# The last layer norm of a fused S5 and attention kernel: Newton's turns on ScalarE, product and sum on VectorE out of PSUM

## The chip, the cores and the metric

The kernel runs on one core of a Trainium2 chip. The metric is the device time of one execution in microseconds, the median of several runs. The engines are named as in the profile: PE (TensorE), PEld (its weight loads), ACT (ScalarE), DVE (VectorE), POOL (GpSimd) and SP (SyncE, which issues the DMAs here).

## The reference

Two sequences of 2048 rows and 512 features go through an S5 block with a feed-forward part, and then through one attention layer with 16 heads, after which comes the layer norm that is changed here. Cut to what matters:

```python
def _sln(h, w, ln_g, ln_b, Wg, bg, Wb, bb):
    mu = jnp.mean(h, axis=-1, keepdims=True)
    var = jnp.mean((h - mu) ** 2, axis=-1, keepdims=True)
    ln = (h - mu) / jnp.sqrt(var + EPS) * ln_g + ln_b
    gamma = (w @ Wg.T + bg)[:, None, :]
    beta = (w @ Wb.T + bb)[:, None, :]
    return gamma * ln + beta

h = _sln(hidden, ...)                       # first norm
q, k, v = ...                               # 16 heads of 32
energy = jnp.einsum('bhqd,bhkd->bhqk', q, k)
att = jax.nn.softmax(energy, axis=-1) / D ** 0.5
out = (att @ v) @ Wp.T + bp
h1 = out + hidden
h2 = _sln(h1, ...)                          # the last norm
return h2 + h1
```

With g = gamma * ln_g and t = gamma * ln_b + beta the last step is, for each row, h1 + t + g * (h1 - mean) / sqrt(var + eps).

## The kernel before

**Attention in blocks and steps.** After the S5 part (about 1.47 ms) attention runs in 64 blocks: 2 batches, 8 pairs of heads, 4 chunks of 512 queries. A block has NP = 8 steps, and step j of the whole loop (j = 8 times the block, plus the step) handles two of the block's 16 key tiles. Ten of the 16 are computed 15 steps ahead (AHEAD): PE writes scores `s` (L754), ACT copies them to a ring (L765, `keep`), DVE keeps their running maximum (L770). The six others only give a maximum at first (`across`: PE m, DVE top L784) and are computed again when they are used (`make`: PE s, DVE adds the shift, pT L819). The negated maximum of each query, `shift`, is turned by PE (`turn_run`, L790 and L791, at steps 2 and 4 of a block; `spread`, L801 and L803, at step 5) and comes back through DRAM. POOL adds it to the kept tiles (`take_off`, L813), ACT takes the exponential (L824), and PE multiplies with v (L834, `weighted`) a step later. PSUM has two buffers `s`, one `m`, one `o` and one bank `pt`, which the turned maxima share with the last part below.

**The last part of the layer** is done per tile of 128 rows, four tiles to a chunk. `fetch` loads the heads' outputs, the divisors and the residual rows; `divide` (POOL, L892) divides; `project` (PE, L905) multiplies with Wp; `residual` (DVE, L911) adds, which gives h; `statistics` (DVE, L917 and L920) takes mean and variance. `deviation`, for two tiles at once (128x2 operands), computes 1/sqrt(var + eps) on DVE: v (L932), a first guess from the bits (L119), three Newton turns of three instructions (L124, L126, L127), and the shift -mean * scale (L938). `last_norm` is an activate on ACT, y = scale * h + shift. `close` on POOL multiplies by g and adds h + t, which `add_t` has left ready (L924, L962, L963), and SP stores the rows.

**Which step it falls in.** The order on every engine is that of the program, which `after(j, ...)` (at the start of step j) and `closing(j, ...)` (at its end, j + 0.5) fill by hand. Batch 0's 16 tiles are worked off while batch 1's attention runs, two in every three blocks: the even tile of a pair starts in one block and the odd one in the next. Their projection uses the bank `pt`. Batch 1 (LB, the last one) has its first three chunks, 12 tiles, at the end of the loop, one tile in every two steps; there the projection uses `m`, and last_norm writes to PSUM (z, L949), DVE multiplies by g (L950), POOL adds t and then the product (L960, L963). Batch 1's last chunk is the tail, `end_last`: four tiles at once, after the last block.

**The tail.** After the projection into py and statistics on DVE, ACT copies py to `hts` (L1057), POOL adds t to each of the four (L1059), while DVE computes the deviations of all four (128x4, L1063 and `rsqrt`). ACT normalises into SBUF (L1069), DVE multiplies by g (L1073), and the sums with hts (L1074) go to DVE and POOL in turn.

Of the kernel before, what the change touches and what calls it, by code (L numbers as in the profile page):

```python
# [8 lines left out]
F32 = mybir.dt.float32  # L9
# [3 lines left out]
I32 = mybir.dt.int32  # L13
AF = mybir.ActivationFunctionType
ALU = mybir.AluOpType
# [4 lines left out]
P = 128  # L20
EPS = 1e-5
# [18 lines left out]
def tile_s5_block_then_sln_attention(  # L40
# [21 lines left out]
    nc = tc.nc  # L62
    NB, L, D = x.shape
    KC = D // P
    CH = 512
    TT = CH // P
# [8 lines left out]
    const = ctx.enter_context(tc.tile_pool(name="const", bufs=1))  # L75
    small = ctx.enter_context(tc.tile_pool(name="small", bufs=2))
# [10 lines left out]
    nc.gpsimd.memset(cond_q, 0.0)  # L87
    nc.gpsimd.tensor_copy(cond_q[:, :, :NB], cond)
    four = const.tile([P, NB], F32, name="four")

    mod = const.tile([P, N_MOD, KC, NB], F32, name="mod")
    u_scale = const.tile([P, KC, NB], F32, name="u_scale")
# [20 lines left out]
        return vec[:, at : at + KC].unsqueeze(2).to_broadcast([P, KC, NB])  # L113


    def rsqrt(v, y, n, turns=(0, 3)):

        if turns[0] == 0:
            nc.vector.tensor_scalar(  # L119
                y.bitcast(I32), v.bitcast(I32), -0.5, float(0x5F3759DF), ALU.mult, ALU.add  # L120
            )
        for _ in range(*turns):
            a = small.tile([P, n], F32, name="rs_a", tag=f"rs_a{n}")
            nc.vector.tensor_mul(a, y, y)  # L124
            b = small.tile([P, n], F32, name="rs_b", tag=f"rs_b{n}")
            nc.vector.scalar_tensor_tensor(b, a, -0.5, v, ALU.mult, ALU.mult)  # L126
            nc.vector.scalar_tensor_tensor(y, b, 1.5, y, ALU.add, ALU.mult)  # L127
# [725 lines left out]
    held, ending = {}, {}  # L853
# [54 lines left out]
    def residual(b, qt):  # L908

        o4, h, py = held[b, qt]  # L910
        nc.vector.tensor_add(h, py, h)  # L911
        held[b, qt] = h, o4.rearrange("p g q -> p (g q)")

    def statistics(b, qt):
        h, ht = held[b, qt]
        st = small.tile([P, 6], F32, name="st3")
        nc.vector.bn_stats(st, h)  # L917
        if qt % 2 == 0:
            held[b, "mv"] = small.tile([P, 2, 2], F32, name="mv3")
        nc.vector.bn_aggr(held[b, "mv"][:, qt % 2, :], st)  # L920

    def add_t(b, qt):
        h, ht, *_ = held[b, qt]
        nc.gpsimd.tensor_tensor(ht, h, ending[b][1], ALU.add)  # L924

    def deviation(b, qt, parts=(0, 1)):

        mv = held[b, "mv"]
        if 0 in parts:
            v = small.tile([P, 2], F32, name="v3")  # L930
            y = small.tile([P, 2], F32, name="scale3", bufs=3)
            nc.vector.tensor_scalar(v, mv[:, :, 1], EPS, None, ALU.add)  # L932
            held[b, "vy"] = v, y
        v, y = held[b, "vy"]
        rsqrt(v, y, 2, {(0,): (0, 1), (1,): (1, 3), (0, 1): (0, 3)}[tuple(parts)])
        if 1 in parts:
            shift = small.tile([P, 2], F32, name="shift3", bufs=3)
            nc.vector.scalar_tensor_tensor(shift, mv[:, :, 0], -1.0, y, ALU.mult, ALU.mult)  # L938
            for i in range(2):
                h, ht = held[b, qt - 1 + i]  # L940
                held[b, qt - 1 + i] = h, ht, y[:, i : i + 1], shift[:, i : i + 1]

    def last_norm(b, qt):

        h, ht, scale, shift = held[b, qt]
        y = work.tile([P, D], F32, name="y")
        if b == LB:
            z = ps.tile([P, CH], F32, name="z", tag="pt")
            nc.scalar.activation(z, h, AF.Identity, bias=shift, scale=scale)  # L949
            nc.vector.tensor_tensor(y, z, ending[b][0], ALU.mult)  # L950
        else:
            nc.scalar.activation(y, h, AF.Identity, bias=shift, scale=scale)
        held[b, qt] = h, ht, y

    def close(b, qt):

        h, ht, y = held.pop((b, qt))
        if b == LB:
            ht = h
            nc.gpsimd.tensor_tensor(h, h, ending[b][1], ALU.add)  # L960
        else:
# [68 lines left out]
    def end_last(o):  # L1030
        raw, inv, on = (spare(n)[:, 0, :] for n in ("raw4", "inv4", "on4"))
        turned = ps.tile([P, 2, 2 * P], F32, name="turned", tag="pt")
        parts = [slice(2 * i * P, 2 * (i + 1) * P) for i in range(2)]
        for at in parts:
            nc.scalar.copy(raw[:, at], o[:, at])
        end_begin(1)
        for i, at in enumerate(parts):
            nc.tensor.matmul(turned[:, i, :], ends["turn"], raw[:, at], start=True, stop=True)  # L1038
        for i, at in enumerate(parts):
            nc.vector.reciprocal(inv[:, at], turned[:, i, :])  # L1040
            nc.vector.tensor_tensor(on[:, at], o[:, at], inv[:, at], ALU.mult)
# [24 lines left out]
        for t in range(TT):  # L1066
            qt = LC * TT + t
            y, ht = ends["h"][t // 2][:, t % 2, :], hts[t // 2][:, t % 2, :]
            nc.scalar.activation(  # L1069
                y, ends["py", t // 2][:, t % 2, :], AF.Identity,  # L1070
                bias=shift[:, t : t + 1], scale=scale[:, t : t + 1],
            )
# [38 lines left out]
    FIRST = -AHEAD - 8  # L1111
    OPEN = -4
    for i, n in enumerate(opens):
        free = NP * (max(m for m in range(N) if pair_of[m] == i - 2) + 1) if i > 1 else FIRST
# [2 lines left out]
    for n in range(N):  # L1117
        after(max(FIRST + 1 + n, NP * n - AHEAD - 6), load_q, n)
        after(NP * n - AHEAD + NP + 1, turn_run, n, 0)
        after(NP * n - AHEAD + NP + 3, turn_run, n, 1)  # L1120
        after(NP * n - AHEAD + NP + 4, spread, n)
    for b in range(NB):
        for c in range(NQ):
            j = NP * (blocks.index((b, NPAIR - 1, c)) + 1) + 1
# [21 lines left out]
            for t in range(TT):  # L1146
                qt = c * TT + t
                if b == LB:
# [30 lines left out]
    def run_due(j):  # L1179
        for what, args in due.pop(j, ()):  # L1180
# [117 lines left out]
```

## Time and profile before

| | |
|---|---|
| median of 3 runs | 3531.95 us (3527.56 to 3532.42) |
| the profiled execution | 3530.68 us, of which the span of the instructions is 3528.9 us |
| mean granted clock of TensorE | 0.983 |
| busy in the span | PE 96%, DVE 63%, ACT 54%, POOL 57% |
| attention and the last part | from about 1472 us to the end |
| batch 0's last part | blocks 34 to 58, about 2455 to 3264 us |
| batch 1's twelve tiles | about 3324 to 3497 us |
| the tail | about 3497 us to the end |

A line of a window names its stretch in us from the start of the span, its length, the busy time and number of instructions of PE, PEld, DVE, ACT and POOL, then the granted clock, the DMA share and GB/s. A line of the timeline has the start, the busy time, engine, line, operation, tiles, shapes and number of instructions merged, and in brackets the idle time of the engine before it with what ended it. A line of a group ends with the busy time, the mean in ns of one instruction, and the idle time before the group.

### The profile page before, as it was taken

The page shows a single profiled execution, that of the slowest core. Times are in us where ns is not written, and L with a number is a line of the kernel's source. Part 1 is how long each engine was busy: PE and PEld are TensorE (multiplying, and loading weights), DVE is VectorE, ACT ScalarE, POOL GpSimd, SP SyncE. Part 2 cuts the span into 40 slices and gives each one's busy share as a digit, 9 for nine tenths or more (in the row PEclk, how much of TensorE's full clock was granted, in tenths as well). Part 3 has the DMA queues.
Part 4 walks back from the last instruction along what each step waited for, and adds up shares of the span by engine and source line. Part 5 has one row for each costly group of instructions (what it writes and reads, how often), then busy time and mean ns, then how long its engine had stood idle before and what let it go on. Part 6 is the DMA issues. An engine that isn't in the chain of part 4 may idle for free. (4 is left out here: it accounts for less than half of the span.)

```text
span 3528.9 us, 34023 instructions
## 1 busy us (share of the span) xinstructions
PE 3382.5 (96%) x11772; PEld 1536.7 (44%) x11772; DVE 2219.1 (63%) x2946; ACT 1899.6 (54%) x2150; POOL 2006.8 (57%) x1028
## 2 busy tenths in 40 slices
PE   7999999999999999899999999999999999999986
PEld 4444444444444444444444444444444444444432
DVE  6233232323232212589999999998888888888865
ACT  2111112111111111488888888888788888888743
POOL 4223131313131311288877888888798888888765
PEclk8999999999999999999999999999999999999988
DMA  8001111111111012332313222232233323323232
GB/s 298 1 30 42 48 39 45 39 49 38 48 36 42 33 43 75 100 71 65 71 48 76 70 66 63 55 72 67 71 83 85 90 71 79 84 71 79 72 92 78
DMA packets 201539, 236.91 MB, mean 67 GB/s; under 512 B 89754, under 2 KB 118938, under 8 KB 197272
## 3 DMA queue, kind: packets, MB, share of 16 engines
q1 hardware_dynamic: 201368, 234.74, 24.4%
q8 instruction: 93, 1.52, 0.2%
q14 instruction: 78, 0.64, 0.1%
HBM read 166.77 MB, written 67.76 MB: 66 GB/s over the span
## 5 line engine op out<-in xcount | busy, mean ns | idle before, releaser
L813 POOL TENSOR_TENSOR x<-x,shift 128x1024 f32<-128x1024 f32 x640 | 1506.6, 2396 | 237.3 <-DMA shift<-flat 177.1
L765 ACT COPY x<-s 128x1024 f32<-128x1024 f32 x640 | 635.3, 1013 | 291.5 <-PE s L754 288.9
L754 PE MATMUL s<-qs,ks 128*128 128x512 f32 x2048 | 699.6, 432 | 48.1 <-DVE run L770 44.3
L824 ACT ACTIVATE x<-x 128x1024 f32<-128x1024 f32 x640 | 676.8, 1058 | 16.5 <-POOL x L813 16.5
L834 PE MATMUL o<-x,v 128*64 128x512 f32 x2560 | 673.4, 622 | 0.6 <-ACT x L824 0.6
L770 DVE TENSOR_TENSOR run<-s,run 128x1024 f32<-128x1024 f32 x512 | 625.2, 1221 | 56.6 <-ACT x L765 39.0
L819 DVE TENSOR_TENSOR pT<-s,shift 128x1024 f32<-128x1024 f32 x384 | 467.5, 1217 | 57.9 <-PE s L754 52.6
L784 DVE TENSOR_REDUCE top<-m 128x1 f32<-128x768 f32 x512 | 486.0, 949 | 25.7 <-PE m L779 25.3
L754 PEld LDWEIGHTS s<-qs,ks 128*128 128x128 f32 x2048 | 346.4, 189 | 303.9 <-DVE run L770 133.2
L488 PE MATMUL ph<-fT,w_sb 128*128 128x512 f32 x1024 | 462.4, 596 | 0.0
L501 PE MATMUL po<-w_sb,hid 128*128 128x512 f32 x1024 | 460.3, 592 | 0.0
L824 ACT ACTIVATE pT<-pT 128x1024 f32<-128x1024 f32 x384 | 407.6, 1061 | 59.2 <-DVE pT L819 51.8
L834 PE MATMUL o<-pT,v 128*64 128x512 f32 x1536 | 399.4, 598 | 13.4 <-ACT pT L824 13.4
L492 ACT ACTIVATE hid<-ph,vec 128x512 f32<-128x512 f32 x128 | 88.1, 688 | 594.8 <-PE ph L488 594.8
L159 DVE SCALAR_TENSOR_TENSOR lo<-pk,vec,hi 128x512 fp32r<-128x512 f32 x64 | 48.1, 751 | 502.7 <-ACT hi L158 497.5
L488 PEld LDWEIGHTS ph<-fT,w_sb 128*128 128x128 f32 x1024 | 192.9, 191 | 228.2 <-issue 228.2
L779 PE MATMUL m<-ks,qs 128*128 128x384 f32 x1024 | 286.1, 361 | 5.2 <-DVE top L784 3.5
L501 PEld LDWEIGHTS po<-w_sb,hid 128*128 128x128 f32 x1024 | 190.7, 190 | 221.5 <-issue 221.5
L435 POOL TENSOR_TENSOR m<-m,m 128x512 f32<-128x512 f32 x8 | 13.1, 1644 | 448.5 <-DVE m L433 448.5
L834 PEld LDWEIGHTS o<-x,v 128*64 128x64 f32 x2560 | 140.1, 137 | 265.2 <-issue 163.0
L158 ACT ACTIVATE hi<-pk,vec 128x512 fp32r<-128x512 f32 x64 | 44.0, 688 | 392.5 <-PE pk L531 392.5
L511 POOL TENSOR_TENSOR x<-x,gated 128x512 f32<-128x512 f32 x32 | 39.6, 1271 | 354.3 <-DVE gated L510 354.3
(249 smaller groups left out, 2844.9 us busy)
## 6 DMA issues: line engine op xcount, KB each, us to landing
ks<-kd SPq DMA_DIRECT2D x128, 256.0 KB
qs<-qd SPq DMA_DIRECT2D x512, 64.0 KB
shift<-flat SPq DMA_DIRECT2D x64, 512.0 KB
x<-in_x SPq DMA_DIRECT2D x8, 1024.0 KB
w_sb<-in_w SPq DMA_DIRECT2D x8, 1024.0 KB
x<-x SPq DMA_DIRECT2D x8, 1024.0 KB
kd<-hi SPq DMA_DIRECT2D x32, 256.0 KB
kd<-lo SPq DMA_DIRECT2D x32, 256.0 KB
```

The source lines that it names most:

```text
L488: nc.tensor.matmul(ph, w1_sb[:, k, f * P : (f + 1) * P], fts[b, c][:, k, :], start=k == 0, stop=k == KC - 1)
L492: nc.scalar.activation(hids[f], ph, AF.Gelu_apprx_tanh, bias=vec[:, V_B1 + f : V_B1 + f + 1], scale=1.0)
L501: nc.tensor.matmul(pos[b, c][:, t, :], hid[:, t * P : (t + 1) * P], w2_sb[:, f, :], start=f == 0, stop=f == FC - 1,)
L754: nc.tensor.matmul(s[:, e, :], kst[pair_of[n], e][:, kt * P : (kt + 1) * P], qst[n][:, e, :], start=True, stop=True,)
L765: nc.scalar.copy(x, s)
L770: nc.vector.tensor_tensor(runs[n], s, kept[n, 0] if kt == 1 else runs[n], ALU.max)
L779: nc.tensor.matmul(m[:, i, :YW], qst[n][:, e, t * P : (t + 1) * P], kst[pair_of[n], e][:, k : k + YW], start=True, stop=True,)
L784: nc.vector.tensor_reduce(tops[n][:, j, 0:1], m[:, :, :YW], AX.XY, ALU.max, negate=True)
L813: nc.gpsimd.tensor_tensor(x, x, shifts[n], ALU.add)
L819: nc.vector.tensor_tensor(x, s, shifts[n], ALU.add)
L824: nc.scalar.activation(x, x, AF.Exp)
L834: nc.tensor.matmul(outs[n][64 * e : 64 * e + 64, :], v[:, kt, e : e + 2, :], x[:, e, :], start=first, stop=final,)
```

## The change

`deviation` and `add_t` go. `statistics` now also computes, per tile on 128x1 operands, v = var + eps, the first guess `y` of the root, v * -0.5, and -mean, all four on DVE. A new function `newton` does the turns on ACT, as three activates each (y squared; times v plus 1.5; times y), and at the end multiplies -mean by the root. `last_norm` writes z to the bank `pt` for every tile. A new function `gain` has DVE multiply z by g in PSUM and add h. `close` keeps one addition on POOL, of t. The steps of these calls are set anew, one tile at a time. `SPREAD` only gives a name to the step at which `spread` already is. In the tail the normalised rows stay in PSUM, DVE multiplies and adds, and t is added last, by POOL for three tiles and by DVE for the fourth.

```diff
     def statistics(b, qt):
...
+        v = small.tile([P, 1], F32, name="v3")
+        y = small.tile([P, 1], F32, name="scale3", bufs=4)
+        shift = small.tile([P, 1], F32, name="shift3", bufs=4)
+        nc.vector.tensor_scalar(v, mv[:, 1:2], EPS, None, ALU.add)
+        nc.vector.tensor_scalar(
+            y.bitcast(I32), v.bitcast(I32), -0.5, float(0x5F3759DF), ALU.mult, ALU.add
+        )
+        nc.vector.tensor_scalar(v, v, -0.5, None, ALU.mult)
+        nc.vector.tensor_scalar(shift, mv[:, 0:1], -1.0, None, ALU.mult)
+        held[b, qt] = h, y, shift, v
+
+    def newton(b, qt, turns, final):
+
+        h, y, shift, v = held[b, qt]
+        for _ in range(turns):
+            c = small.tile([P, 1], F32, name="c3")
+            nc.scalar.activation(c, y, AF.Identity, scale=y)
+            nc.scalar.activation(c, c, AF.Identity, bias=one_half, scale=v)
+            nc.scalar.activation(y, c, AF.Identity, scale=y)
+        if final:
+            nc.scalar.activation(shift, shift, AF.Identity, scale=y)
 
     def last_norm(b, qt):
...
+        h, scale, shift, _ = held[b, qt]
+        z = ps.tile([P, CH], F32, name="z", tag="pt")
+        nc.scalar.activation(z, h, AF.Identity, bias=shift, scale=scale)
+        held[b, qt] = h, z
+
+    def gain(b, qt):
+
+        h, z = held[b, qt]
+        nc.vector.tensor_tensor(z, z, ending[b][0], ALU.mult)
+        nc.vector.tensor_tensor(h, z, h, ALU.add)
 
     def close(b, qt):
 
-        h, ht, y = held.pop((b, qt))
-        if b == LB:
-            ht = h
-            nc.gpsimd.tensor_tensor(h, h, ending[b][1], ALU.add)
-        else:
-            nc.gpsimd.tensor_tensor(y, y, ending[b][0], ALU.mult)
-        nc.gpsimd.tensor_tensor(y, y, ht, ALU.add)
-        nc.sync.dma_start(out[b, qt * P : (qt + 1) * P, :], y)
+        h, z = held.pop((b, qt))
+        nc.gpsimd.tensor_tensor(h, h, ending[b][1], ALU.add)
+        nc.sync.dma_start(out[b, qt * P : (qt + 1) * P, :], h)
...
             nc.scalar.copy(hts[i], ends["py", i])
-            for t in range(2):
-                nc.gpsimd.tensor_tensor(hts[i][:, t, :], hts[i][:, t, :], t_row, ALU.add)
...
         for t in range(TT):
+            z = ends["py", t // 2][:, t % 2, :]
+            nc.scalar.activation(
+                z, z, AF.Identity, bias=shift[:, t : t + 1], scale=scale[:, t : t + 1]
+            )
+        for t in range(TT):
             qt = LC * TT + t
...
-            nc.vector.tensor_tensor(y, y, g_row, ALU.mult)
-            (nc.gpsimd if t % 2 else nc.vector).tensor_tensor(y, y, ht, ALU.add)
+            y, z = hts[t // 2][:, t % 2, :], ends["py", t // 2][:, t % 2, :]
+            nc.vector.tensor_tensor(z, z, g_row, ALU.mult)
+            nc.vector.tensor_tensor(y, z, y, ALU.add)
+            (nc.gpsimd if t < TT - 1 else nc.vector).tensor_tensor(y, y, t_row, ALU.add)
...
                     after(k + 3, statistics, b, qt)
-                    if t % 2:
-                        after(k + 4, deviation, b, qt)
-                        after(k + 5, last_norm, b, qt - 1)
-                        closing(k + 5, last_norm, b, qt)
-                        after(k + 6, close, b, qt - 1)
-                        closing(k + 6, close, b, qt)
+                    closing(k + 3, newton, b, qt, 2, False)
+                    closing(k + 4, newton, b, qt, 1, True)
+                    closing(k + 4, last_norm, b, qt)
+
+                    (after if (k + 5 - SPREAD) % NP == 0 else closing)(k + 5, gain, b, qt)
+                    closing(k + 6, close, b, qt)
                 else:
...
                     closing(k + 7, statistics, b, qt)
-                    after(k + 9, add_t, b, qt)
-                    if t % 2:
-                        closing(k + 8, deviation, b, qt, (0,))
-                        closing(k + 9, deviation, b, qt, (1,))
-                        closing(k + 10, last_norm, b, qt - 1)
-                        closing(k + 11, last_norm, b, qt)
-                        after(k + 12, close, b, qt - 1)
-                        after(k + 14, close, b, qt)
+                    for i in range(3):
+                        closing(k + 8 + i, newton, b, qt, 1, i == 2)
+
+                    k += 2 if t % 2 else 8
+                    closing(k + 10, last_norm, b, qt)
+                    closing(k + 11, gain, b, qt)
+                    after(k + 13, close, b, qt)
```

In batch 0 k is step 3 of the tile's own block. The turns of a tile stand at the ends of steps 3, 4 and 5 of the block after its own. The two z of a pair stand in the same block, the one after the odd tile's own: the even tile's at the end of step 5, the odd tile's at the end of step 7. Each gain stands one step behind its z.

More of the change, by code (lines that the diff above doesn't have):

```diff
@@ L89, in tile_s5_block_then_sln_attention @@
     four = const.tile([P, NB], F32, name="four")
+    one_half = const.tile([P, 1], F32, name="one_half")
+    nc.gpsimd.memset(one_half, 1.5)
     mod = const.tile([P, N_MOD, KC, NB], F32, name="mod")
@@ L113, in per_feature, with rsqrt @@
         return vec[:, at : at + KC].unsqueeze(2).to_broadcast([P, KC, NB])
[L116 to L122, printed above, removed]
+    def rsqrt(v, y, n):
+        nc.vector.tensor_scalar(
+            y.bitcast(I32), v.bitcast(I32), -0.5, float(0x5F3759DF), ALU.mult, ALU.add
+        )
+        for _ in range(3):
             a = small.tile([P, n], F32, name="rs_a", tag=f"rs_a{n}")
@@ L911, in residual @@
         nc.vector.tensor_add(h, py, h)
-        held[b, qt] = h, o4.rearrange("p g q -> p (g q)")
+        held[b, qt] = h
     def statistics(b, qt):
-        h, ht = held[b, qt]
+        h = held[b, qt]
         st = small.tile([P, 6], F32, name="st3")
         nc.vector.bn_stats(st, h)
[L918 to L941, printed above, removed]
@@ L943, in last_norm @@
-    def last_norm(b, qt):
-        h, ht, scale, shift = held[b, qt]
-        y = work.tile([P, D], F32, name="y")
-        if b == LB:
-            z = ps.tile([P, CH], F32, name="z", tag="pt")
-            nc.scalar.activation(z, h, AF.Identity, bias=shift, scale=scale)
-            nc.vector.tensor_tensor(y, z, ending[b][0], ALU.mult)
-        else:
-            nc.scalar.activation(y, h, AF.Identity, bias=shift, scale=scale)
-        held[b, qt] = h, ht, y
-    def close(b, qt):
-        h, ht, y = held.pop((b, qt))
-        if b == LB:
-            ht = h
-            nc.gpsimd.tensor_tensor(h, h, ending[b][1], ALU.add)
-        else:
-            nc.gpsimd.tensor_tensor(y, y, ending[b][0], ALU.mult)
-        nc.gpsimd.tensor_tensor(y, y, ht, ALU.add)
-        nc.sync.dma_start(out[b, qt * P : (qt + 1) * P, :], y)
+        mv = small.tile([P, 2], F32, name="mv3")
@@ new lines, in statistics @@
+        nc.vector.bn_aggr(mv, st)
+        v = small.tile([P, 1], F32, name="v3")
+        y = small.tile([P, 1], F32, name="scale3", bufs=4)
+        shift = small.tile([P, 1], F32, name="shift3", bufs=4)
+        nc.vector.tensor_scalar(v, mv[:, 1:2], EPS, None, ALU.add)
+        nc.vector.tensor_scalar(
+            y.bitcast(I32), v.bitcast(I32), -0.5, float(0x5F3759DF), ALU.mult, ALU.add
+        )
+        nc.vector.tensor_scalar(v, v, -0.5, None, ALU.mult)
+        nc.vector.tensor_scalar(shift, mv[:, 0:1], -1.0, None, ALU.mult)
@@ L1066, in end_last @@
         for t in range(TT):
-            qt = LC * TT + t
[L1068 to L1072, printed above, removed]
-            nc.vector.tensor_tensor(y, y, g_row, ALU.mult)
-            (nc.gpsimd if t % 2 else nc.vector).tensor_tensor(y, y, ht, ALU.add)
+            z = ends["py", t // 2][:, t % 2, :]
+            nc.scalar.activation(
+                z, z, AF.Identity, bias=shift[:, t : t + 1], scale=scale[:, t : t + 1]
+            )
+        for t in range(TT):
+            qt = LC * TT + t
+            y, z = hts[t // 2][:, t % 2, :], ends["py", t // 2][:, t % 2, :]
+            nc.vector.tensor_tensor(z, z, g_row, ALU.mult)
+            nc.vector.tensor_tensor(y, z, y, ALU.add)
+            (nc.gpsimd if t < TT - 1 else nc.vector).tensor_tensor(y, y, t_row, ALU.add)
             nc.sync.dma_start(out[LB, qt * P : (qt + 1) * P, :], y)
@@ L1111, in tile_s5_block_then_sln_attention @@
     FIRST = -AHEAD - 8
+    SPREAD = -3
     OPEN = -4
@@ L1120, in tile_s5_block_then_sln_attention @@
         after(NP * n - AHEAD + NP + 3, turn_run, n, 1)
-        after(NP * n - AHEAD + NP + 4, spread, n)
+        after(NP * n + SPREAD, spread, n)
     for b in range(NB):
```

## The prediction

> **What bounds the kernel now.** I read the page first: PE is busy 96% of the span, GpSimd only 57%, so shortening GpSimd's work is worth something only where PE waits for it, directly or through another engine. Next the windows, one block of attention each: an undisturbed block, then the blocks with the even tile's projection, the odd tile's projection, and the end of the pair's last norm.
>
> ```profile
> 2225.30:2254.10 28.80, 28.27 (x123) 12.82 (x122) 26.19 (x27) 25.71 (x28) 23.51 (x10) 1.00 0.15 42
> 2682.80:2714.70 31.90, 31.57 (x130) 14.27 (x129) 27.17 (x30) 25.91 (x28) 28.22 (x14) 1.00 0.58 128
> 2714.70:2746.90 32.20, 30.49 (x126) 13.39 (x124) 27.33 (x34) 25.90 (x28) 25.91 (x12) 1.00 0.14 38
> 2746.90:2778.70 31.80, 30.38 (x127) 13.56 (x127) 29.01 (x35) 27.09 (x30) 26.21 (x14) 1.00 0.46 96
> ```
>
> The columns after the length are busy PE, PEld, DVE, ACT, POOL. A clean block takes 28.8 us with PE busy for all but 0.5 of it; a projection adds 3.05 us of PE. So the third window should take 31.85 and the fourth, which has no projection, 28.8: it takes 31.8. Counted from one first L784 of a block to the next in DVE's timeline, the eight blocks that hold a pair's norm take 32.07 (2732.21 to 2764.29) to 34.74 us, 33.15 on average, 4.36 more than a clean one: 35 us in batch 0. The even tile's block takes 32.12.
>
> Then the groups and DVE's timeline, for what costs so much. v (L932) is a 128x2 instruction of 0.15 us that takes 1.38 on average:
>
> ```profile
> L932 DVE TENSOR_SCALAR v<-mv 128x2 f32<-128x2 f32 x12 | 16.5, 1377 | 0.0
> ...
> 3403.07 7.00 POOL L813 TENSOR_TENSOR x<-x,shift 128x1024 f32<-128x1024 f32 x3
> ...
> 3404.49 0.97 DVE L932 TENSOR_SCALAR v<-mv 128x2 f32<-128x2 f32 x1
> ...
> 3405.50 2.28 DVE L119 TENSOR_SCALAR scale<-v 128x2 int32<-128x2 int32 x1
> ...
> 3407.82 2.27 DVE L124 TENSOR_TENSOR rs_a<-scale 128x2 f32<-128x2 f32 x1
> ...
> 3410.13 0.16 DVE L126 SCALAR_TENSOR_TENSOR rs_b<-rs_a,v 128x2 f32<-128x2 f32 x1
> ...
> 3413.08 1.06 ACT L824 ACTIVATE pT<-pT 128x1024 f32<-128x1024 f32 x1 [7.25 <-DVE pT L819]
> ...
> 3414.19 1.08 PE L834 MATMUL o<-pT,v 128*64 128x512 f32 x4 [2.92 <-ACT pT L824]
> ```
>
> Each of these DVE instructions ends where a GpSimd instruction ends (7.00/3 = 2.33 us each); when GpSimd is out of work, the next one takes 0.16. Behind the chain stands pT, and ACT and PE stand behind pT.
>
> The third thing is how tightly a clean block is coupled. PE writes a tile of scores s, ACT copies it (L765), DVE takes the running maximum (L770), and only then PE may write that buffer again. The step with two copies, from the timeline of a clean block:
>
> ```profile
> 2220.98 1.93 ACT L765 COPY x<-s 128x1024 f32<-128x1024 f32 x2 [0.29 <-PE s L754]
> 2222.02 2.55 DVE L770 TENSOR_TENSOR run<-s,run 128x1024 f32<-128x1024 f32 x2
> ...
> 2223.30 0.73 PE L754 MATMUL s<-qs,ks 128*128 128x512 f32 x2
> ...
> 2224.63 0.72 PE L754 MATMUL s<-qs,ks 128*128 128x512 f32 x2 [0.25 <-DVE run L770]
> ```
>
> The first run starts as its copy ends (2220.98 + 1.01), and each s of PE starts as a run ends. ACT idled only 0.29 us before. What is put ahead of that copy on ACT, or ahead of that run on DVE, delays PE almost one to one; elsewhere in the block ACT has 0.3 to 0.8 us a step.
>
> **What the Trainium skill says.** "GPSIMD Engine Reference", 1. Specifications: GpSimd shares its SBUF interfaces with VectorE, which shows with instructions in a 2-port mode or with two SBUF inputs. The trace agrees: L119 and L124 wait out GpSimd, while L911, L819 and L770 (one input in PSUM) keep 0.68 and 1.2 us beside it. "ScalarE: Activation LUTs", What ACT_TABLE_LOAD costs: 186 ns plus 0.833 ns an element, about 93 ns for each [128,1] pointer operand. L952 with two pointers agrees (price 0.80, trace 0.805 us). "TensorE: Matmul & The Clock Gate", Part 1: the array's clock drops after idle windows; the windows after 3400 us show 0.82 to 0.88.
>
> **The change, part by part.** PE's order is the same before and after.
>
> 1. *Deviation leaves DVE.* Per pair go 12 small instructions, 11 x 0.195 (0.16 and a gap of 0.035) = 2.15 and v's 1.38. Per tile come four 128x1 ones (v, first guess, -0.5 v, -mean): 4 x 0.19 = 0.76. The trace has no 128x1 tensor_scalar beside GpSimd; the nearest is last (L453), a 128x1 copy beside L461, 0.15 us, with no wait. Bounds 0.6 to 8 us a tile; I take 0.76.
>
> 2. *Newton on ACT.* Three dependent 128x1 activates a turn, with one, two and one pointers: 0.28 + 0.37 + 0.28, plus gaps of 0.035 as on DVE: about 1.03 us, an estimate from the skill's price; 0.28 more for the last shift. No such row is in the trace; bounds 0.7 and 1.6 a turn. 28 tiles x 3.4 = 95 us more on ACT, of which most falls on idle ACT, but not all: see 5.
>
> 3. *Product and sum on DVE out of PSUM.* Two of 0.69 us (L950 has 690 ns) per tile, neither with two SBUF inputs. They hold the one pt bank from z on; the next user is turn_run at least half a step later, so I see no wait there.
>
> 4. *GpSimd* keeps one of three 1.29 us instructions a tile: 16 x 2.58 + 12 x 1.27 = 57 us less. Worth nothing in batch 0: GpSimd runs ahead there and stands 9.2 us per pair for y (L962); it will stand for the gain instead, some 4 us later in the block, with two more take_offs done before. On SP as many out-DMAs as before (0.3 us each) wait for it, the odd tile's now behind the next fetch; loads have steps to spare.
>
> 5. *Batch 0, even tile's block* (now 32.12 us). The step counted is the one with two copies. Its first copy starts 10.14 us into a clean block (2220.98 less 2210.84). In the step before, pT now comes behind residual, statistics and the four small ones, so the exp behind it ends at about 9.8 (before 9.2); then turn 1 of 1.03 and the next exp of 0.96: copy at 11.8. Run L770 is then 1.65 us later than in a clean block instead of 0.43, and PE's next s starts when it ends. The later turns fall into steps with a projection, where ACT has 1.3 us spare. Loss 1.2 us x 8 = 10.
>
> 6. *Odd tile's block* (now 33.15). The same 1.65; then turn 2 and turn 3 with shift and the even z (0.77) overrun ACT's slack in steps 5 and 6 by about 1.3; the even gain (1.38 less slack) delays step 8 by about 1.2. The odd gain falls where DVE waits 1.27 us for pt_run and costs nothing; without that cover it costs 1.4. Sum 4.1 to 4.2 against 4.36 now: -0.2 x 8 = -2. Batch 0 together: **+8 us**, from -10 to +20.
>
> 7. *Batch 1's twelve tiles* (3324 to 3497 us). From residual (L911) to residual a tile takes 11.1 to 17.0 us. While scores are still kept (five tiles, 68.1 us), the chain is projection 3.7, then DVE: residual 0.69, statistics 0.87, small 0.76, pT 1.13, top 0.86, run 1.15, gain 1.3, pT and top 2.0: 12.5 a tile, -5.5. Afterwards (six, 79.5 us) the intervals with a deviation take 13.2 to 17.0 and two without 10.2. I take 11.3, since exp now stands behind statistics and two turns (2.1 us): -11.7. The last pair's stall: -2. Together **-19**, from -8 to -27.
>
> 8. *Tail.* L1059's adds go, and with them the waits of v, guess, rs_a and rs_b: 0.28 + 1.02 + 1.02 + 1.02 = 3.35 us. Then z 0.81, eight DVE instructions of 0.65, one add of 0.69 after GpSimd's third: the last sum ends at 3522.1 instead of 3525.9: **-3.8**.
>
> Sum: 8 - 19 - 3.8 = -15. The profiled execution took 3530.68 (span 3528.9 and 1.8 around it); the median shown is 1.3 above. So 3531.95 - 15 = **3517**.
>
> **Rivals.**
> - *Slower: ACT's turns decide.* The place is L765 behind a turn in batch 0, the price 4 turns' worth per pair (one in the even block, three in the odd) x 8 = 32 us for each 1 us that a turn takes over 1.03. From 1.5 us a turn nothing is left of the 15; at 1.7 it is slower by over 7. For it: ACT is 89% busy in a clean block. Against: the price of pointers fitted L952. At 1.8: 3541.
> - *Slower by far: 128x1 tensor_scalars wait for GpSimd too.* Three waits of 2.3 us and half a one, 8 us a tile, 16 tiles: near 3640. L453 speaks against it.
> - *Faster than I say.* Row slack swallows ACT's turns (as the even block swallowed 1.56 us of residual and statistics for 0.41): batch 0 at -10, batch 1 at -25: 3493.
> - *Nothing to measure.* Projection, residual and the m bank set batch 1's pace whatever DVE does (two intervals without a deviation took 14.4 and 14.9): -8 there, -3.8, +8: 3528.
>
> **How the numbers follow.** A measurement of this kernel tells about 0.2% (7 us) from no change. My forecast (3503 to 3525) 0.45, faster than that 0.22, nothing 0.15, ACT's turns 0.12, tensor_scalar waits 0.06. So faster 0.67, same 0.15, slower 0.18. The range 3494 to 3541 leaves out the far rival and the ends.
>
> **What would show it.** c, scale and shift as 128x1 rows on ACT near 0.3 us; v at 0.15 us with GpSimd running; blocks of batch 0 near 33.3 and 32.9 us; residuals of batch 1 at most 13 us apart; no GpSimd in the 8 us before the last z. Wrong would be v near 1.4 us or more, ACT waited for by run L770 throughout batch 0 with blocks over 35, or residuals still 14 apart.

## The result, and the profile after

The kernel after takes 3533.14 us (median of 20 runs, 3529.99 to 3535.05); the kernel before, run beside it, 3529.53 us (20 runs). The ratio is 1.0009, with a 95% interval from 1.0002 to 1.0016: 3 us slower, where the forecast was 15 faster. The profiled span went from 3528.9 to 3531.7 us. Measured on the two traces, part by part (a step starts with its first exponential on ACT):

| | predicted | measured | from |
|---|---|---|---|
| batch 0's last part | +8 | +8.5 | first top (L784, after: L785) of block 36 to the start of step 487: 855.98 and 864.5 us |
| batch 1's twelve tiles | -19 | -3.0 | start of step 487 to start of step 511: 162.3 and 159.3 us |
| the end | -3.8 | -3.7 | start of step 511 to the end: 37.2 and 33.6 us |

The first top of block 36 also comes 1.0 us later (2474.3 us in place of 2473.3), ahead of everything that was changed in attention; in the traces of all runs below it lies between 2472.0 and 2476.1. So two rows were met in their sums, and the row of batch 1 holds 16 of the 18 us by which the forecast was missed. (Lines after the tiles' code have moved: L784 is L785 in the kernel after, L790 is L791, L801 is L802, L905 is L906, L911 is L912.)

**Batch 0.** The windows of the kernel after for the blocks shown of before, cut at the same places (about 1.4 us behind the start of steps 325, 333, 341 and 349): the even tile's projection, then the odd tile's, then the rest of the pair's norm (columns as explained above):

```profile
2684.90:2719.10 34.20, 33.17 (x136) 14.78 (x137) 29.06 (x35) 27.97 (x35) 27.19 (x13) 1.00 0.50 120
2719.10:2752.20 33.10, 32.08 (x133) 14.27 (x129) 28.14 (x34) 28.41 (x39) 23.45 (x10) 1.00 0.13 37
2752.20:2782.90 30.70, 27.97 (x119) 12.19 (x115) 27.60 (x30) 27.80 (x34) 24.73 (x12) 1.00 0.41 99
```

Read the fourth number after the length: ACT is busy 28.0, 28.4 and 27.8 us, where it was 25.9, 25.9 and 27.1, and its instructions rise from 28, 28 and 30 to 35, 39 and 34. The three lengths sum to 98.0 us, 2.1 more than the 95.9 of before. This pair was the cheapest one before: over the eight pairs, from first top to first top, three blocks take 98.03 us now and took 96.97 before, 1.1 more, or 8.5 in all. Counted so, the even tile's block takes 33.16 us (before 32.12). The odd tile's block takes 34.5 in every pair, where it was anything from 32.1 to 34.7 (33.2 on average); but the block behind it takes 30.4 us and not 31.7, so that nearly all of that loss comes back.

**The prices.** From the groups of the kernel after (instructions, busy time and mean in ns, then idle time ahead of the group):

```profile
L939 ACT ACTIVATE c<-c,one_half,v 128x1 f32<-128x1 f32 x84 | 32.5, 387 | 2.8
L940 ACT ACTIVATE scale<-c,scale 128x1 f32<-128x1 f32 x84 | 24.8, 295 | 2.7
L938 ACT ACTIVATE c<-scale 128x1 f32<-128x1 f32 x84 | 23.8, 283 | 0.4
...
L954 DVE TENSOR_TENSOR z<-z,g_row 128x512 f32<-128x512 f32 x28 | 19.3, 691 | 11.0 <-ACT z L948 11.0
...
L802 PE MATMUL pt_neg<-ident,neg 128*8 128x128 f32 x64 | 17.6, 276 | 7.7 <-DVE xr L955 7.7
...
L925 DVE TENSOR_SCALAR v<-mv 128x1 f32<-128x1 f32 x28 | 4.3, 154 | 1.0
```

A turn is 283 + 387 + 295 ns and two gaps of about 30: 1.03 us, as worked out. v takes 154 ns on average over all 28 tiles, where the 128x2 form took 1377: no wait for GpSimd. What the prediction didn't have are the last figures of L954 and L802, the idle time: DVE stands 11.0 us for z, and PE 7.7 us for xr of `gain`.

**Batch 1.** The windows from step 487 to step 511, before and then after:

```profile
3329.30:3491.60 162.30, 132.80 (x403) 50.70 (x403) 105.81 (x169) 69.87 (x78) 113.02 (x69) 0.88 0.35 96
```

```profile
3338.80:3498.10 159.30, 128.00 (x408) 50.17 (x410) 87.93 (x158) 107.15 (x199) 102.56 (x61) 0.95 0.33 100
```

DVE was relieved of 17.9 us and POOL of 10.5; ACT got 37.3 more. None of the relief reached PE: its idle time is 162.3 - 132.8 = 29.5 us before and 31.3 after. The 3 us gained come from PE's busy time, which is 4.8 us less at a granted clock of 0.95 in place of 0.88. The waits of PE in the two stretches say what changed places:

```profile
PE o L834 <- ACT pT L824: 13.4, 6, 5.6
PE pt_run L790 <- DVE y L950: 8.2, 2, 6.1
PE py L905 <- DVE top L784: 5.4, 2, 3.4
```

```profile
PE pt_run L791 <- DVE xr L955: 10.2, 4, 3.5
PE pt_neg L802 <- DVE xr L955: 7.7, 2, 4.7
PE o L835 <- ACT pT L825: 3.8, 3, 1.5
PE py L906 <- POOL o L893: 2.8, 1, 2.8
```

The waits for pT (13.4 us, the deviation's chain) fell to 3.8, as foreseen. In their place the waits for the bank pt grew: before, PE stood 8.2 us in `turn_run` for y (L950), which read z from that bank; now it stands 17.9 us in `turn_run` and `spread` until `gain` has let go of it. How such a wait comes about is seen in the timeline, at the first of them:

```profile
3355.86 0.15 DVE L925 TENSOR_SCALAR v<-mv 128x1 f32<-128x1 f32 x1
...
3356.37 1.22 DVE L820 TENSOR_TENSOR pT<-s,shift 128x1024 f32<-128x1024 f32 x1
3357.51 0.95 DVE L785 TENSOR_REDUCE top<-m 128x1 f32<-128x768 f32 x1
...
3358.37 0.69 DVE L954 TENSOR_TENSOR z<-z,g_row 128x512 f32<-128x512 f32 x1
3359.09 0.69 DVE L955 TENSOR_TENSOR xr<-z,xr 128x512 f32<-128x512 f32 x1
...
3359.84 0.66 PE L791 MATMUL pt_run<-ident,run 128*128 128x128 f32 x4 [1.94 <-DVE xr L955]
```

z had been written by 3354.8. Its product starts 3.6 us later, because the next tile's residual, statistics and small instructions, pT and top stand ahead of it on DVE. At the longest wait the other end is late too:

```profile
3430.00 1.99 ACT L825 ACTIVATE x<-x 128x1024 f32<-128x1024 f32 x2
3431.90 0.28 ACT L938 ACTIVATE c<-scale 128x1 f32<-128x1 f32 x1
...
3433.28 0.78 ACT L948 ACTIVATE z<-xr,shift,scale 128x512 f32<-128x512 f32 x1
3434.10 0.70 DVE L954 TENSOR_TENSOR z<-z,g_row 128x512 f32<-128x512 f32 x1 [4.07 <-ACT z L948]
...
3435.67 0.37 PE L802 MATMUL pt_neg<-ident,neg 128*8 128x128 f32 x1 [4.70 <-DVE xr L955]
3435.84 5.84 PE L906 MATMUL py<-wp,o 128*128 128x512 f32 x8
...
3441.77 0.69 DVE L912 TENSOR_TENSOR xr<-py,xr 128x512 f32<-128x512 f32 x1 [6.24 <-PE py L906]
```

The last turn stands behind two exponentials, z behind the turn, `gain` behind z, and `spread` behind `gain`. The projection that follows the idle time takes 5.84 us, where others take 3.70.

### The profile page after: what moved, and what is told of

Read it like the earlier page. It is cut to its first block, busy times and chain, and to the rows that moved or that the text cites. A ratio compares the mean times of both kernels' runs of the same rounds, so it can differ in the third digit from the quotient of the medians.

```text
span 3531.7 us, 34142 instructions
## 1 busy us (share of the span) xinstructions
PE 3378.7 (96%) x11772; PEld 1534.2 (43%) x11772; DVE 2204.6 (62%) x2937; ACT 1976.7 (56%) x2430; POOL 1943.5 (55%) x982
## 4 chain that ended last, share of the span: by engine, by line
PE 71%; DVE 14%; ACT 11%; issue 2%; DMA 1%; POOL 1%; SPq 0%; DVEq 0%; ACTq 0%; POOLq 0%
PE o L835 14%; PE ph L489 13%; PE po L502 12%; PE s L755 9%; DVE run L771 8%; PE pk L532 6%; ACT x L766 4%; PE pv L544 3%; PE py L906 3%; ACT x L825 3%; PE m L780 2%; ACT pT L825 2%; DVE pT L820 2%; PE pt_run L791 2%; PE pu L423 2%
## 5 line engine op out<-in xcount | busy, mean ns | idle before, releaser
L835 PE MATMUL o<-x,v 128*64 128x512 f32 x2560 | 664.2, 614 | 2.0 <-ACT raw L844 2.0
L785 DVE TENSOR_REDUCE top<-m 128x1 f32<-128x768 f32 x512 | 485.8, 949 | 25.7 <-PE m L780 25.4
L780 PE MATMUL m<-ks,qs 128*128 128x384 f32 x1024 | 285.8, 360 | 16.3 <-DVE top L785 14.4
```

Of the source, the lines that this page charges most:

```text
L780: nc.tensor.matmul(m[:, i, :YW], qst[n][:, e, t * P : (t + 1) * P], kst[pair_of[n], e][:, k : k + YW], start=True, stop=True,)
L785: nc.vector.tensor_reduce(tops[n][:, j, 0:1], m[:, :, :YW], AX.XY, ALU.max, negate=True)
L835: nc.tensor.matmul(outs[n][64 * e : 64 * e + 64, :], v[:, kt, e : e + 2, :], x[:, e, :], start=first, stop=final,)
```

## The theories

- **A: the bank pt.** z holds it until `gain`, whose place on DVE is late; PE stands in `turn_run` (steps 490, 492, 498, 500) and `spread` (493, 501).
- **B: the turns on ACT.** They stand ahead of copies and exponentials, and make z late.
- **C: the fetched tiles.** POOL's divide waits for its divisors, and PE for POOL (2.8 us above). No run changed the fetches, so C stays untested; PE's waits for POOL's divide in this stretch are at most 3.5 us in any of the traces below.

All runs, in us against the kernel before (ratio less 1, times its median), with the two halves of batch 1 from their traces:

| run | ratio and interval | us | steps 487 to 496 | 497 to 510 |
|---|---|---|---|---|
| before | 1 | 0 | 70.3 | 92.1 |
| after | 1.0009 (1.0002 to 1.0016) | +3 | 73.9 | 85.5 |
| b0_before | 0.9979 (0.9972 to 0.9987) | -7 | 75.4 | 83.7 |
| b1_before | 1.0021 (1.0014 to 1.0028) | +7 | 68.6 | 92.3 |
| z_in_s | 0.9989 (0.9981 to 0.9997) | -4 | 73.9 | 76.9 |
| turns_dve | 0.9991 (0.9985 to 0.9998) | -3 | 74.7 | 79.4 |
| z_sooner | 1.0026 (1.0019 to 1.0034) | +9 | 78.1 | 84.4 |
| z_sooner_dve | 1.0005 (0.9997 to 1.0013) | +2 | 78.6 | 88.9 |
| no_turns_b1 | 0.9994 (0.9986 to 1.0002) | -2 | 68.9 | 82.5 |
| no_turns_zs | 0.9973 (0.9963 to 0.9983) | -10 | 71.0 | 73.9 |
| b0_before_zs | 0.9959 (0.9947 to 0.9972) | -14 | 75.4 | 78.9 |
| b0_before_zs_dve | 0.9965 (0.9951 to 0.9978) | -12 | 73.8 | 72.2 |
| eight_new | 0.9959 (0.9946 to 0.9971) | -14 | 74.2 | 75.2 |
| eight_new_dve | 0.9952 (0.9940 to 0.9964) | -17 | 73.0 | 73.6 |
| turns_in_s | 0.9971 (0.9960 to 0.9981) | -10 | 66.5 | 77.4 |
| turns_in_s_no | 0.9966 (0.9953 to 0.9978) | -12 | 64.3 | 76.4 |
| b0_before_ts_dve | 0.9949 (0.9935 to 0.9962) | -18 | 70.9 | 72.6 |

Each half is read from one trace. Where two kernels have the same code in this stretch, their halves differ by up to 1.8 us (b1_before and before: 68.6 and 70.3; b0_before and after: 83.7 and 85.5), so a smaller difference says nothing.

## The experiments

**1. One batch left as it was.** In `b0_before` batch 0, in `b1_before` batch 1's twelve tiles call the functions of the kernel before at its steps; the rest is new.

> Batch 0 as before the change, batch 1's twelve tiles and the tail as after it. The prediction gave these two parts -19 and -3.8, together -23 us against the kernel before. The traces of before and after gave -3.0 (start of step 487 to start of step 511) and -3.7, together -6.7 us. Theory: what batch 1 lost has its cause in batch 1 itself (the one pt bank, held by z), so the parts add: -5 to -9 us. Rival: batch 0's new norm leaves batch 1 a worse start (POOL and the queues in another state at step 487): then -12 us or more.

> Batch 1's twelve tiles as before the change, batch 0 and the tail as after it. If the parts add: +8.6 in batch 0 and -3.7 in the tail, +5 us against the kernel before, that is 1 to 2 us slower than after. If batch 1's gain was there and batch 0's loss was larger than the row lengths say, this one is slower: +10 or more.

Without batch 0's part the kernel is 7 us faster than before, within the 5 to 9 expected, and batch 1 takes 159.1 us from step 487 to 511, as in the kernel after (159.3): batch 1's loss is its own. With batch 1 left as it was it is 7 us slower (interval 5 to 10, expected 5), and its trace gives batch 0's last part 864.5 us, as in after. Batch 0's new norm costs, as predicted, about 8 us.

**2. z out of pt (z_in_s).**

```diff
-        z = ps.tile([P, CH], F32, name="z", tag="pt")
+        if b == LB and qt >= TT:
+            z = ps.tile([P, 2, CH], F32, name="z", tag="s", bufs=2)[:, 0, :]
+        else:
+            z = ps.tile([P, CH], F32, name="z", tag="pt")
```

> As after, but z of the last eight of batch 1's twelve tiles lies in a buffer s in place of the bank pt; nothing else is changed. Theory A (pt held by z): PE's waits for gain in front of turn_run and spread at steps 498, 500 and 501 (1.8, 3.0 and 4.7 us in after) go, and the start of step 511 comes 7 to 10 us earlier than in after: about -5 us against the kernel before. Theory B (the turns on ACT stand in front of copies and exponentials): the time is lost elsewhere, at most 2 us come back. Theory C (the fetched tiles come too late): likewise at most 2 us. If z in s keeps make from its buffer, pT comes later and nothing is gained: within 2 us of after or slower.

Steps 497 to 510 took 76.9 us in place of 85.5: 8.5 us came back, within the 7 to 10 of theory A, against at most 2 of B and C. The first half, where the edit does nothing, stayed at 73.9.

**3. The turns on DVE (turns_dve).**

```diff
-            nc.scalar.activation(c, y, AF.Identity, scale=y)
-            nc.scalar.activation(c, c, AF.Identity, bias=one_half, scale=v)
-            nc.scalar.activation(y, c, AF.Identity, scale=y)
+            nc.vector.tensor_scalar(c, y, y, v, ALU.mult, ALU.mult)
+            nc.vector.tensor_scalar(y, c, 1.5, y, ALU.add, ALU.mult)
         if final:
-            nc.scalar.activation(shift, shift, AF.Identity, scale=y)
+            nc.vector.tensor_scalar(shift, shift, y, None, ALU.mult)
```

> As after, but the turns are on DVE, at the same steps, as two 128x1 instructions each (y*y*v, then plus 1.5 times y, both pointers per partition) and one for the last shift: 7 x 0.19 = 1.35 us more on DVE and 3.4 us less on ACT for each tile. Theory B (ACT's queue): batch 0's 8.6 us come back but for 2 or 3, and the waits of run for a copy in batch 1 fall, together 8 to 12 us less than after. Theory A: z comes about 1.3 us sooner after the turns, so the waits for pt shrink a little; batch 0 gains as above, batch 1 1 or 2 us. Rival: DVE's 128x1 instructions with pointers wait for GpSimd: 2.3 us each, 20 us or more slower than after.

It is 6 us faster than after, less than the 8 to 12 that B expected, and in part for other reasons. (Its trace is of an execution 2.6 us below the median of its runs; parts read from it sum to more than 6.) In batch 0 a pair takes 97.3 us in place of 98.0, still more than before; 6 us less in all. The even tile's block did not move: 33.2 us with the turns on either engine. So ACT's turn was not its whole cause: 0.65 us of its loss stands a step earlier, ahead of any turn, where the four small instructions delay pT, top and PE's next m (that step grew from 3.92 to 4.57 us in both); the other 0.4 us comes with the turn, on whichever engine. In batch 1 the first half did not gain either; the second gained 6 us, while PE still waited 10.7 us for pt in `turn_run`. What changed with it is that z comes in time: DVE's wait for it fell from 11.0 to 2.6 us, and PE's in `spread` from 7.7 to 3.5. The rival is refuted by the timeline of this kernel, in a block of batch 0:

```profile
2710.15 0.26 DVE L938 TENSOR_SCALAR c<-scale,v 128x1 f32<-128x1 f32 x1
2710.21 2.37 POOL L814 TENSOR_TENSOR x<-x,shift 128x1024 f32<-128x1024 f32 x1
...
2710.45 0.21 DVE L939 TENSOR_SCALAR scale<-c,scale 128x1 f32<-128x1 f32 x1
```

L939 starts and ends inside GpSimd's instruction and did not wait, where the 128x2 forms of before took up to 2.28 us. The groups of the whole trace say the same:

```profile
L938 DVE TENSOR_SCALAR c<-scale,v 128x1 f32<-128x1 f32 x84 | 22.2, 264 | 0.5
L939 DVE TENSOR_SCALAR scale<-c,scale 128x1 f32<-128x1 f32 x84 | 18.0, 214 | 3.0
```

**4. z and gain sooner (z_sooner, and z_sooner_dve with the turns on DVE and batch 0 as before).**

```diff
-                    closing(k + 3, newton, b, qt, 2, False)
-                    closing(k + 4, newton, b, qt, 1, True)
-                    closing(k + 4, last_norm, b, qt)
-
-                    (after if (k + 5 - SPREAD) % NP == 0 else closing)(k + 5, gain, b, qt)
-                    closing(k + 6, close, b, qt)
+                    closing(k + 3, newton, b, qt, 3, True)
+                    after(k + 4, last_norm, b, qt)
+                    closing(k + 4, gain, b, qt)
+                    closing(k + 5, close, b, qt)
```

> As after, but in batch 1 all three turns stand at the end of the tile's own step, z at the start of the next and gain at its end; after has z half a step later and gain a whole step later, behind the next tile's residual, statistics, pT, top and run. z stays in pt, the turns stay on ACT. Theory A (pt held by z behind DVE's queue): all of PE's waits for gain go, those of the first five tiles too (1.9, 3.5 and 3.0 us, besides the 1.8, 3.0 and 4.7 of the last eight); step 487 to 511 takes 145 to 151 us in place of 159.3; -5 to -11 us against the kernel before. Theory B (ACT's queue): three turns at once ahead of each even step, of which 488 and 492 have two copies, cost more than two and one: 157 us or more, within 3 us of after.

> Batch 0 as before the change, the tail as after it. In batch 1 the turns are on DVE (six 128x1 instructions and one for the shift, right behind statistics), z on ACT at the start of the next step, gain at its end; z in pt. Theory A: no wait of PE for gain, no turns in ACT's queue: step 487 to 511 takes 143 to 150 us, the whole -16 to -23 us against the kernel before. Rival: DVE's 1.4 us more in the step of residual and statistics delay pT and top there, and PE through m and s, by 1 us a tile: 155 to 160 us, -8 to -11.

Here theory A failed as a recipe. PE's waits for `gain` in `turn_run` went (10.2 us to none), but the stretch took 162.4 us, on B's side (157 or more), and the kernel became 9 us slower than before, which is more than B had. The waits of DVE in batch 1 show why:

```profile
DVE z L954 <- ACT z L948: 27.0, 6, 5.3
...
DVE run L771 <- ACT x L766: 16.9, 5, 4.4
```

DVE now stands 27.0 us for z (11.0 in after) and 16.9 us for the copies behind three turns (4.4 in after); in `spread`'s steps PE still stands, 11.3 us. The steps alternate between 8 to 14 and 2 to 7 us: what was spread over two is now a chain inside one. With the turns on DVE, right behind the statistics (z_sooner_dve), the whole stretch took 167.5 us, not the 143 to 150 expected, nor the rival's 155 to 160: ACT waits 68.2 us for pT, which stands behind residual, statistics and eleven small instructions. A place that is right for the bank can be wrong for the queue.

**5. The turns left out (no_turns_b1), and with z in s as well (no_turns_zs).**

```diff
-                    closing(k + 3, newton, b, qt, 2, False)
-                    closing(k + 4, newton, b, qt, 1, True)
+                    closing(k + 3, newton, b, qt, 0, False)
+                    closing(k + 4, newton, b, qt, 0, True)
```

> As after, but in batch 1's twelve tiles Newton's turns are left out (the first guess of the root is used as it is), only the shift's product stays on ACT; the steps of z and gain are those of after. Theory A (gain's place behind DVE's other work decides when pt is free): PE's waits for gain in front of turn_run stay within a third of their length, DVE's waits for z go; step 487 to 511 takes 153 to 158 us in place of 159.3. Theory B (3.1 us of turns a tile on ACT were the loss): 145 to 150 us.

> As after, with both edits at once: z of the last eight tiles in a buffer s, and Newton's turns left out in batch 1 (the first guess is used as it is). From step 487 to 511 after takes 159.3 us; z in s alone took 150.8 (-8.5), the turns left out alone 151.3 (-8.0). If the bank pt and ACT's turns are two separate losses, they add: 142 to 145 us, which is what the prediction had (162.3 - 19 = 143), and -11 to -15 us against the kernel before. If both only took away the same wait in turn: 148 to 151 us, -4 to -7.

Without turns the stretch took 151.3 us, between the two theories' numbers and nearer B's; PE's waits in `turn_run` stayed (11.0 us), as A said, and DVE's wait for z fell from 11.0 to 3.5. Both edits together took 144.9 us: of 8.0 + 8.5 us, 14.4 came, so as long as pt still holds the first tiles they are two losses for the most part (experiment 7 lowers the turns' share). Against before the whole gained 10 us (6 to 13), a little under the 11 to 15 expected.

**6. Which version is best (b0_before_zs, b0_before_zs_dve, eight_new, eight_new_dve).** All four leave batch 0 as before and have z of the last eight tiles in s; `dve` has batch 1's turns on DVE; `eight_new` leaves the first four tiles too as before.

> Batch 0 as before the change, batch 1's twelve tiles and the tail as after it, with z of the last eight of the twelve tiles in a buffer s in place of pt. Run apart, the two edits gave -7.4 us against the kernel before (batch 0 left as it was) and -7.1 against after (z in s; 8.5 in the trace from step 487 to 511). If they add: -14 to -16 us against the kernel before. If the wait for pt only goes because batch 0's new norm shifts the queues: -7 to -9.

> As the run with batch 0 as before and z in s (-14.4 us), but the turns of batch 1 on DVE, six 128x1 instructions and one for the shift at the same steps. In the last eight tiles turns on DVE gave 79.4 us against 85.5 of after while pt was still the bank of z; with z in s I expect 71 to 76 us there (77 to 79 with ACT's turns), in the first five tiles 74 to 76 us as before: -16 to -20 us against the kernel before. If DVE's own queue is the bound once pt is free: 78 us or more, no better than -14.

> As the run with batch 0 as before and z in s (-14.4 us), but the first four of batch 1's twelve tiles too are left as before the change; only the last eight tiles and the tail are new. Steps 487 to 496 took 70.3 us in the kernel before and 73.9 to 75.4 with the new norm; steps 497 to 510 with z in s 77 to 79. If the new norm loses in the first tiles because ACT still copies scores there: 70 to 72 and 77 to 80 us, -16 to -20 us against the kernel before. If the loss there only moves behind step 496: -13 to -15.

> As the run before this one, with the last eight tiles' turns on DVE. 70 to 72 us in steps 487 to 496 and 71 to 76 in steps 497 to 510: -20 to -26 us against the kernel before. If DVE is the bound there: no better than with ACT's turns.

The first added up: -14 us. The second has the expected halves, 73.8 and 72.2, but its five timed runs gave only -12 (8 to 17), short of the 16 to 20 expected; its trace is of an execution 7 us below their median. `eight_new` missed: the first half took 74.2 us and not 70 to 72. Its steps 487 to 493 are those of before, but step 495, in which the new way begins, grew from 9.2 to 11.9: the loss moved to the seam, and the whole is at -14, as the second of the two expectations had it. With turns on DVE it was -17 (13 to 21), short of the 20 to 26 expected.

**7. The transposes out of pt (turns_in_s, turns_in_s_no, b0_before_ts_dve).** z keeps pt in all twelve tiles; `turn_run` and `spread` of the last two blocks go to a buffer s. This reaches the first tiles too.

```diff
-        pt = ps.tile([P, TT, P], F32, name="pt_run", tag="pt")
+        if n >= N - 2:
+            pt = ps.tile([P, 2, TT, P], F32, name="pt_run", tag="s", bufs=2)[:, 0]
+        else:
+            pt = ps.tile([P, TT, P], F32, name="pt_run", tag="pt")
...
+        if n >= N - 2:
+            pt = ps.tile([P, 2, CH], F32, name="pt_neg", tag="s", bufs=2)[:, 0, :]
+        else:
```

> As after, but turn_run and spread of the last two blocks use a buffer s, so that z keeps pt to itself in all twelve tiles; the turns stay on ACT. If pt also costs the first tiles: steps 487 to 496 take 66 to 70 us in place of 73.9 (PE's waits of 5.4 and 3.0 us there go), 497 to 510 take 76 to 79 in place of 85.5; -7 to -12 us against the kernel before. If the first tiles' pace is that of ACT and of s, which now has three more users there: 73 to 76 us, and -2 to -5.

> The same with Newton's turns left out in batch 1 (the first guess is used as it is). With pt free and no turns on ACT the prediction's sum should hold in the first tiles too: 70.3 - 5.5 = 65 us for steps 487 to 496 (63 to 67), and 73 to 76 for steps 497 to 510; -15 to -20 us against the kernel before. If s with its three more users is the bound there: 69 to 72 and 73 to 76, -9 to -13, as with z in s and no turns.

> Batch 0 as before the change, all of batch 1's twelve tiles new with the turns on DVE, the tail new, and turn_run and spread of the last two blocks in a buffer s. With z in s in their place steps 487 to 496 took 73.8 us and 497 to 510 72.2 (-12 us against the kernel before, interval 8 to 17). If pt costs the first tiles: 68 to 71 and 71 to 74 us, -17 to -22. If not: the same as with z in s.

Nothing of the norm, its steps or its engines is changed in `turns_in_s`, and 66.5 + 77.4 = 143.9 us is 15.4 less than the kernel after needs; both halves lie in the ranges expected if pt also costs the first tiles. The window from step 487 to 511, and PE's waits in it that concern the transposes:

```profile
3339.50:3483.50 144.00, 126.88 (x408) 49.02 (x410) 87.58 (x158) 106.87 (x200) 102.60 (x61) 0.96 0.38 110
```

```profile
PE s L755 <- DVE top L795: 2.3, 2, 1.2
...
PE pt_run L794 <- DVE pT L826: 0.2, 1, 0.2
```

The engines are as busy as in after (ACT 106.9, DVE 87.6), but PE idles 17.1 us in place of 31.3, and of the 17.9 us for pt only these 2.5 stand there now; the waits for pT rose from 3.8 to 7.4. Without the turns as well it took 140.7: with pt free the turns cost 3.2 us, not 8.0. So more than half of their price had been that z came late to a bank others were waiting for. (The whole of that run gained 12 us, short of the 15 to 20 expected.) The third run, with batch 0 as before and the turns on DVE, has the lowest median of all, 3509.06 us (five runs) against 3528.97: 18 us (13 to 23) faster than before, as expected, and 21 than after, by the ratios; the interval of eight_new_dve overlaps with it. Its stretch takes 143.5 us, no less than with the turns on ACT (143.9): with pt free it made no difference there which engine has the turns. Batch 0 as before together with pt free and the turns on ACT was not run.

## Why the prediction was wrong

Nearly all of the miss lies in the sum of item 7, and its cause is one clause of item 3.

- **Items 1 and 2, the prices: right.** 0.15 us for each 128x1 on DVE without a wait, 1.03 us a turn; the trace of before had neither form.
- **Item 3 is the step that failed**: "the next user is turn_run at least half a step later, so I see no wait there." The half step was counted in the order of the program and put into the sum as zero, though DVE and ACT had work between z and `gain`. In fact `gain` stands at the end of step 489, behind all of DVE's work of that step, and `turn_run` at the start of 490, with no work of DVE between; and `spread` at 493 and 501 shares its step with a `gain`. PE stood 17.9 us there, and taking those users off pt, alone, gave 15.4 us back. In batch 0 the clause held: no wait of PE for `gain` stands in that part of the trace of after. A warning stood in the trace of before: PE's 8.2 us in `turn_run` for y (L950), the reader of z in the same bank.
- **Item 7 inherits it.** It summed the chain of a tile with `gain` as 1.3 us of DVE's time and no wait of PE for it. With pt free its sum holds: -19 predicted, 162.3 - 143.9 = -18.4 measured. For the first half it had 70.3 - 5.5 = 64.8 us: 66.5 with the turns on ACT, 64.3 without. Turns ahead of the step's copies were left out of that half's sum; run waited 4.4 us for copies in after (1.3 in before, 0.2 without turns). Three residuals of batch 1 stand 14.4, 18.6 and 20.8 us behind the one before, a sign of failure that the prediction had named.
- **Items 5 and 6, batch 0: right in sum** (+8 and +8.5), by blocks +1.04 for the even one (+1.2 expected) and about 0 for the odd one (-0.2 expected): +1.35 in the odd tile's own block, -1.3 in the one behind it, which the prediction did not count. The even block's cause was named with both parts, the small instructions and the turn; experiment 3 shows the first to be the larger.
- **Item 8, the tail: the total is right by luck.** From the tail's first copy to the last sum it fell from 29.4 to 26.9 us, -2.5; the rest of the 3.7 is step 511, which the item did not count. The waits of v, guess, rs_a and rs_b went as worked out (v to shift: 5.67 to 2.33 us), but two terms were short:

```profile
3520.58 2.99 ACT L1063 ACTIVATE py<-py,shift,scale 128x512 f32<-128x512 f32 x4 [1.64 <-DVE shift L1060]
...
3522.15 0.70 DVE L1069 TENSOR_TENSOR py<-py,g_row 128x512 f32<-128x512 f32 x1 [1.66 <-ACT py L1063]
...
3527.86 0.69 DVE L1071 TENSOR_TENSOR ht<-ht,t_row 128x512 f32<-128x512 f32 x1
```

The first product starts 1.57 us behind the first z, when two z are written and not one (0.81 was taken; that two tiles share one py is the likely reason, which no run isolates), and the eight instructions take 5.7 us, not 5.2.
- **The rivals.** "Nothing to measure" had the nearest time (3528) and the wrong mechanism: projection, residual and m did not set the pace, as 143.9 us with all three in place shows. "ACT's turns decide" had the right sign, but its place was batch 0 and its condition a turn of 1.5 us or more, which did not hold. (Its own price, 32 us for each us over 1.03, gives 6 us slower at 1.7, not over 7.) GpSimd did not hold up the 128x1 instructions, and batch 0 did not swallow the turns.

## What to carry to other kernels

When a result is parked in a buffer that others share, price the holding time by the queue of the engine that frees it: list what stands ahead of the freeing instruction on its queue, and what stands ahead of the one that fills the buffer. Here the prices of the new instructions in the tiles were right, and one shared bank ate 15 of 19 us. And before moving the holder, try to move the other users: giving six calls of the transposes another buffer took the wait away for 2.3 us of waits at that buffer, while an earlier z only handed it on.

## What was not expected of the hardware

In the trace of turns_dve a 128x1 tensor_scalar with per-partition pointers took 0.21 to 0.26 us on DVE beside a running GpSimd instruction, where 128x2 forms without pointers waited up to 2.3 us in before: two such instructions make a Newton turn in about 0.5 us, half of ACT's 1.03. And idle time came with a slower clock: after PE had stood 4.7 us, the granted clock from 3433.5 to 3440.3 us was 0.50, and the eight matmuls of the projection in that stretch took 5.84 us in place of 3.70.
